# Moving the cross scores' maxima, two bfloat16 roundings and an output norm off ScalarE and VectorE

## The chip, the cores and the metric

The kernel runs on one core of a Trainium2 chip. Its five engines are TensorE (PE, whose weight loads are listed apart as PEld), VectorE (DVE), ScalarE (ACT), GpSimd (POOL) and SyncE (SP), which here only issues DMAs. The metric is device time in microseconds (us) of one launch; lower is better.

## The reference

One decoder layer with three sublayers, each followed by a residual and a layer norm, for 32 sequences ("batches") of 256 tokens by 256 features in float32:

```
x = layernorm(x + self_attention(x))         # 16 query heads of 64, 4 key/value heads, RoPE, ALiBi
x = layernorm(x + cross_attention(x, ctx))   # 16 heads of 16
x = layernorm(x + ffn(x))                    # bit-linear: weights in {-1, 0, 1}, activations rounded to 8 bits
```

Cross attention norms each of q, k, v and its own output before the projection (weight, bias), and lets each query see the keys of its own and the previous window of 64 that have the same cell id. Its heart, for one head:

```
p = where(mask, q @ k.T / sqrt(16), lowest)
a = exp(p - max(p)) / sum(exp(p - max(p)))
o = a @ v
y = (layernorm(o) * w + b) @ w_o.T + b_o
```

## The kernel before, in words

**Order of work.** Everything is unrolled in Python. Time is cut into slots of about 4 us, four to a group; a batch starts every 16 slots. In one group PE does two self-attention units of the current batch (scores L393, transposes L471, values L492) and one cross-attention unit of the batch before (scores L674, transposes L713, values L729, back-transposes L749). Generators (`self_inputs`, `self_output`, `cross_inputs`, `cross_output`, `feed_forward`) give the rest and yield until a later slot. For PE, DVE and ACT the program order is kept as written (`manual_schedule`); the order on POOL and on SP, which are not in that list, is made by the tile framework's scheduler when the program is built. Every engine works its own queue strictly in order.

**A cross unit.** Four heads lie in one 128x512 tile `xp`, and a unit has two such halves, with 128 queries and 128 keys for each head. DVE (L688) takes the scores from PSUM, adds the mask, negates, writes `xp` and gives each row's minimum to `xnm`, eight instructions to a unit. ACT (L704, `cross_exp`) then does one exponential for each head, with `xnm` as its bias operand and scale -1. PE transposes (L713), ACT copies (L715, `xpT`), PE multiplies with the values (L729); the value tiles have a column of ones, which gives the sum. There are four units to a batch.

**The queries of a cross unit** (`xqT`) come, for each half of the tokens, from `self_output`: PE `wo` (L513), DVE residual and statistics, POOL `rs_x` (L528 to L531), DVE `row` (L538), PE transposes (L204 `zqT`), projection (L550), ACT bias (L568 `qb`), an SP DMA that swaps neighbouring rows (L573), and POOL's rotation (L584, L585, L586). The keys `kTz` come by eight small SP DMAs (L658).

**Self attention's side jobs on DVE, POOL and SP.** The reciprocal sums are spread by a DVE copy `wide` (L443), a transposing SP DMA `planes` (L448) and a POOL copy `R` (L455). The rotary embedding needs four SP DMAs for each 128x512 tile (L312, `other<-psin`) and a POOL add (L354, `qT` or `kT`).

**Feed forward.** POOL scales and rounds (L803 `tr`, L852 `gu`), adding a large constant; DVE subtracts it again and writes bfloat16 (L805 `xib`, L855 `hib`); SP transposes by DMA (L809 `xiT`, L857 `hiT`); PE multiplies (L816, L863).

**Cross output.** DVE statistics of `on`, POOL `rstd_zo` (three small instructions, L184 to L186), ACT scales and shifts `on` (L198), PE transposes (L204 `zoT`) and multiplies with `xo_w` (L775), DVE adds the residual (L779).

Of the kernel before, what the change touches and what calls it, by code (L numbers as in the profile page):

```python
# [10 lines left out]
BF16 = mybir.dt.bfloat16  # L11
I32 = mybir.dt.int32
U16 = mybir.dt.uint16
AF = mybir.ActivationFunctionType
ALU = mybir.AluOpType
AX = mybir.AxisListType

P = 128
L = 256
NT = L // P  # L20
D = 256
NDC = D // P
EPS = 1e-5
# [7 lines left out]
XHH = 4  # L31
XE = XHD + 1
K_, V_, Q_, O_ = range(4)

INNER = 1024
# [3 lines left out]
MAGIC = 12582912.0  # L39
# [12 lines left out]
def kernel(  # L52
# [27 lines left out]
    nc = tc.nc  # L80
# [5 lines left out]
    def ctile(shape, dtype, name):  # L86
        return const.tile(shape, dtype, name=name, tag=name)
# [3 lines left out]
    def bank(name, shape=(P, 512), dtype=F32):  # L91
        return ps.tile(list(shape), dtype, tag="b", name=name)
# [4 lines left out]
    neg_half = ctile([P, 2], F32, "neg_half")  # L97
# [5 lines left out]
    def work(name, shape, bufs=2, dtype=F32):  # L103
        return sb.tile(list(shape), dtype, tag=name, name=name, bufs=bufs)

    def small(name, n):
        return sb.tile([P, 8], F32, tag="small", name=name, bufs=48)[:, 0:n]
# [36 lines left out]
    ones = ctile([P, P], F32, "ones")  # L144
# [10 lines left out]
    for i in range(2):  # L155


        t = ctile([P, (NT + 1) * XH * XE + 32 - XE], F32, f"xvaug{i}")
# [14 lines left out]
    def stats(src, name):  # L173

        st = small("st", 6)
        mv = small(f"mv_{name}", 2)
        nc.vector.bn_stats(st, src)
        nc.vector.bn_aggr(mv, st)
        return mv

    def rstd_of(mv, name):

        rb = small(f"rstd_{name}", 2)
        nc.gpsimd.tensor_scalar(rb[:, 0:1], mv[:, 1:2], EPS, None, ALU.add)  # L184
        nc.gpsimd.tensor_tensor(rb[:, 0:1], rb[:, 0:1], neg_half[:, 0:1], ALU.pow)
        nc.gpsimd.tensor_scalar(rb[:, 1:2], mv[:, 0:1], rb[:, 0:1], -1.0, ALU.mult, ALU.mult)  # L186
        return rb


    last = []  # L190
# [9 lines left out]
    def transposed(dst, src, name):  # L200

        pt = bank(name)
        for dc in range(NDC):
            nc.tensor.transpose(pt[:, dc * P : (dc + 1) * P], src[:, dc * P : (dc + 1) * P], ident)  # L204
        nc.scalar.copy(dst, pt[:, 0 : NDC * P].rearrange("p (c t) -> p c t", t=P))


    def prepare_cross():


        nc.sync.dma_start(vecs_sb, vecs)
        nc.sync.dma_start(cols_sb, cols)
        for j, (w, dst) in enumerate(
            (
                (wxk, xkv_w[:, :, 0:D]),
                (wxv, xkv_w[:, :, D : 2 * D]),
                (wxq, xq_w),
                (wxo, xo_w),
            )
        ):  # L220
            raw = work("tr", [P, NDC, D], 3)
            nc.sync.dma_start(raw, w.rearrange("(c p) n -> p c n", p=P))
            for dc in range(NDC):
                nc.gpsimd.tensor_scalar(
                    dst[:, dc, :], raw[:, dc, :], vecs_sb[:, j, 0, dc : dc + 1], None, ALU.mult
                )
            if j == 0:
                nc.sync.dma_start(wo_sb, Wo.rearrange("(c p) n -> p c n", p=P))
            if j in xbias:
                more = work("xp", [P, 512])  # L230
                row = more[:, 0:D]
                nc.sync.dma_start(row, rows[j].partition_broadcast(P))
                for dc in range(NDC):
                    nc.gpsimd.tensor_scalar(
                        more[:, D + dc * P : D + (dc + 1) * P],
                        ones,
                        vecs_sb[:, j, 1, dc : dc + 1],
                        None,
                        ALU.mult,
                    )  # L240
            yield 2
            pb = bank("mm")
            if j in xbias:
                for dc in range(NDC):
                    nc.tensor.matmul(
                        pb[:, 0:D],
                        more[:, D + dc * P : D + (dc + 1) * P],
                        raw[:, dc, :],
                        start=(dc == 0),
                        stop=(dc == NDC - 1),  # L250
                    )
                nc.vector.tensor_tensor(xbias[j], pb[:, 0:D], row, ALU.add)
            else:
                for ch in range(NDC):
                    for dc in range(NDC):
                        nc.tensor.matmul(
                            pb[:, ch : ch + 1],
                            raw[:, dc, ch * P : (ch + 1) * P],
                            vecs_sb[:, j, 1, dc : dc + 1],
                            start=(dc == 0),  # L260
                            stop=(dc == NDC - 1),
                        )
                nc.vector.tensor_tensor(xbcol[j], pb[:, 0:NDC], cols_sb[:, j, :], ALU.add)
            yield 2
# [401 lines left out]
    def cross_scores(b, i):  # L666
# [16 lines left out]
        for half in range(2):  # L683
            s["xp", i, half] = p = work("xp", [P, 512])
            for j in range(XHH):
# [10 lines left out]
                    s["xnm", i][half][:, j : j + 1],  # L696
                )

    def cross_exp(b, i, half):
        s = state[b]  # L700
        p = s["xp", i, half]
        for j in range(XHH):
            cols = slice(j * P, (j + 1) * P)
            nc.scalar.activation(  # L704
                p[:, cols], p[:, cols], AF.Exp, bias=s["xnm", i][half][:, j : j + 1], scale=-1.0
            )

    def cross_turn(b, i, half):
        s = state[b]
# [52 lines left out]
    def cross_output(b, t):  # L762
        s = state[b]
        on = s["on", t]
        mv = stats(on, "zo")
        rstd = rstd_of(mv, "zo")
        yield
        last.append(partial(scaled, on, on, rstd))
        yield 2
        zoT = work("zT", [P, NDC, P])  # L770
        transposed(zoT, on, "zoT")
        yield 2
        py = bank("xw")
        for dc in range(NDC):
            nc.tensor.matmul(py[:, 0:D], zoT[:, dc, :], xo_w[:, dc, :], start=(dc == 0), stop=(dc == NDC - 1))  # L775
        if t == 0:
            s["x2"] = work("x2", [P, NT, D])
        h = s["x2"][:, t, :]
        nc.vector.tensor_tensor(h, py[:, 0:D], s["x1", t], ALU.add)  # L779
        mv = stats(h, "x2")  # L780
        rstd = rstd_of(mv, "x2")
        yield
        last.append(partial(scaled, h, h, rstd))


    def feed_forward(b):
        x2 = state[b]["x2"]

        s = small("ffs", NT)
# [10 lines left out]
        xi = work("tr", [P, NT, D], 3)  # L800
        xib = work("xib", [P, NT, D], 1, BF16)
        for t in range(NT):
            nc.gpsimd.tensor_scalar(xi[:, t, :], x2[:, t, :], up[:, t : t + 1], MAGIC, ALU.mult, ALU.add)  # L803
        yield
        nc.vector.tensor_scalar(xib, xi, MAGIC, None, ALU.subtract)  # L805

        xiT = work("xiT", [P, NT, NDC, P], 1, BF16)
        for t in range(NT):
# [2 lines left out]
        gu = work("gu", [P, NT, INNER], 1)  # L811
# [14 lines left out]
        for t in range(NT):  # L826
            for half in range(2):
                pg = hidden("gate", t, half)
                cols = gu[:, t, half * 512 : (half + 1) * 512]
# [3 lines left out]
        for t in range(NT):  # L833
            for half in range(2):
                pg = hidden("up", t, half)
                cols = gu[:, t, half * 512 : (half + 1) * 512]
# [3 lines left out]
        for t in range(NT):  # L840

            m = small("ffm", 1)
            nc.vector.tensor_reduce(m, gu[:, t, :], AX.X, ALU.max, apply_absolute_value=True)
            sh = small("ffsh", 1)
            nc.vector.tensor_scalar(sh, m, u_of[:, t : t + 1], QUANT_MIN, ALU.mult, ALU.max)
            hup = small("ffhup", 1)
            nc.vector.reciprocal(hup, sh)
            nc.vector.tensor_scalar(hup, hup, u_of[:, t : t + 1], 127.0, ALU.mult, ALU.mult)
            d_of = small("ffd", 1)
            nc.vector.tensor_scalar(d_of, sh, ff_scale["down"], None, ALU.mult)  # L850
            d_ofs.append(d_of)
            nc.gpsimd.tensor_scalar(gu[:, t, :], gu[:, t, :], hup, MAGIC, ALU.mult, ALU.add)  # L852
            yield
            hib = work("hib", [P, INNER], 2, BF16)
            nc.vector.tensor_scalar(hib, gu[:, t, :], MAGIC, None, ALU.subtract)  # L855
            hiT = work("hiT", [P, NIC, P], 2, BF16)
            nc.sync.dma_start_transpose(hiT, hib)  # L857
            hiTs.append(hiT)
        yield 2
        for t in range(NT):  # L860
            py = bank("ffo")
# [6 lines left out]
            mv = stats(y, "y")  # L868
            rstd = rstd_of(mv, "y")
# [16 lines left out]
    at(-16, self_inputs(0))  # L886
    at(-16, prepare_buffers())
    at(-15, prepare_cross())
    at(2, prepare_ffn())
    for b in range(B):  # L890
        s0 = 16 * b
        if b:
            at(s0 - 15, self_inputs(b))
        at(s0 + 2, cross_inputs(b))
        for t in range(NT):
            at(s0 + 9 + 8 * t, self_output(b, t))
            at(s0 + 4 * CROSS + 11 + 8 * t, cross_output(b, t))
        at(s0 + 4 * CROSS + 26, feed_forward(b))

    with tc.manual_schedule(engines={mybir.EngineType.PE, mybir.EngineType.DVE, mybir.EngineType.Activation}):  # L900
        running = []
        slot = min(starts)
        while starts or running:
            m, part = divmod(slot, 4)
            k = m - CROSS
# [147 lines left out]
```

## Time and profile before

| what | value |
|---|---|
| median of 3 runs (lowest, highest) | 2186.22 us (2183.72, 2188.77) |
| span of the profiled execution, first to last instruction | 2184.1 us |
| busy: PE, DVE, ACT, POOL | 96%, 81%, 73%, 59% of the span |
| ACT: the cross exponentials L704 | 1024 of 416 ns, 331.8 us |
| DVE: `hib` L855 and `xib` L805 | 64 of 908 ns and 32 of 1384 ns |
| granted PE clock, mean | 0.983 |

The page gives no time of the profiled execution beside its span; the runs' median is 2.1 us above the span, and that is taken as what lies around it. Busy times are sums of instruction durations, so an instruction that waits for a port inside its duration counts as busy. In a timeline the columns are start, duration, engine, line, operation, output<-input with shapes, count, and in brackets the idle time before it with what ended that. Line numbers are those of the kernel before.

### The profile page before, as it was taken

How to read it: one execution, taken by the hardware profiler on the slowest of the kernel's cores; microseconds unless marked ns; L12 is line 12 of the kernel's file. 1: busy time of each engine (PE TensorE's matmuls, PEld its weight loads, DVE VectorE, ACT ScalarE, POOL GpSimd, SP SyncE). 2: the span in 40 equal slices, each digit the busy share in tenths (PEclk: the TensorE clock that was granted, in tenths of full speed). 3: DMA queues.
4: the chain of work that ended last, by engine and by line, in shares of the span. 5: the costliest groups of instructions: out<-in, count | busy, mean ns of one | idle time of the engine just before them, and what ended most of it. 6: DMA issues, size and time to landing. Idle time of an engine off the chain costs nothing.

```text
span 2184.1 us, 54367 instructions
## 1 busy us (share of the span) xinstructions
PE 2096.9 (96%) x17316; PEld 1606.7 (74%) x17316; DVE 1778.0 (81%) x6949; ACT 1600.0 (73%) x4833; POOL 1285.1 (59%) x1977
## 2 busy tenths in 40 slices
PE   7899999999999999999999999999999999999983
PEld 5677777777777777777777777777777777777751
DVE  4777888888888888888888888888888888888765
ACT  2478778777778877777877777877777877777862
POOL 4555665566655656655656655656666566666542
PEclk9899999999999999999999999999999999999986
DMA  7432333333333334334334333333343333333211
GB/s 219 111 75 72 82 75 83 77 79 86 89 72 78 83 71 91 86 71 86 76 76 89 82 77 79 78 81 83 86 82 76 81 82 74 90 81 69 53 42 32
DMA packets 326589, 177.57 MB, mean 81 GB/s; under 512 B 242976, under 2 KB 296096, under 8 KB 326304
## 3 DMA queue, kind: packets, MB, share of 16 engines
q1 hardware_dynamic: 324608, 170.52, 34.6%
q8 instruction: 139, 2.28, 0.5%
q10 hardware_dynamic: 1696, 3.57, 0.5%
q14 instruction: 146, 1.20, 0.2%
HBM read 39.50 MB, written 8.39 MB: 22 GB/s over the span
## 4 chain that ended last, share of the span: by engine, by line
PE 74%; DVE 11%; ACT 5%; POOL 4%; DMA 4%; issue 1%; SPq 0%; ACTq 0%; POOLq 0%; DVEq 0%
PE wo L513 10%; PE o L492 8%; PE proj L330 8%; PE t L471 8%; PE s L393 8%; PE ff L816 5%; PE xt L713 4%; PE xo L729 3%; PE xq L550 3%; PE xs L674 3%; PE ffo L863 3%; PE xk L622 3%; DVE p L409 2%; PE xw L775 2%; PE v L362 2%; DVE xib L805 2%
## 5 line engine op out<-in xcount | busy, mean ns | idle before, releaser
L427 ACT ACTIVATE p<-p,nm 128x256 f32<-128x256 f32 x1024 | 511.6, 512 | 197.7 <-DVE nm L409 197.7
L409 DVE CUSTOM_DVE_ANT_0 p<-s,alibi 128x256 f32<-128x256 f32 x1024 | 364.6, 416 | 6.3 <-PE s L393 6.3
L480 ACT COPY pT<-t 128x512 f32<-128x512 f32 x512 | 276.1, 601 | 89.6 <-PE t L471 89.3
L704 ACT ACTIVATE xp<-xp,xnm 128x128 f32<-128x128 f32 x1024 | 331.8, 416 | 0.0
L688 DVE CUSTOM_DVE_ANT_0 xp<-xs,mask 128x128 f32<-128x128 f32 x1024 | 225.9, 285 | 68.1 <-PE xs L674 68.1
L455 POOL COPY R<-planes 128x1024 uint16<-128x1024 uint16 x128 | 175.4, 1370 | 176.3 <-DMA planes<-wide 164.6
L471 PE MATMUL t<-ident,p 128*128 128x128 f32 x2048 | 266.4, 273 | 0.9 <-ACT p L427 0.9
L492 PE MATMUL o<-pT,v 128*64 128x256 f32 x2048 | 260.8, 386 | 1.3 <-ACT pT L480 1.1
L393 PE MATMUL s<-kT,qT 64*128 64x256 f32 x2048 | 255.7, 389 | 0.0
L513 PE MATMUL wo<-wo_sb,oT 128*128 128x256 f32 x1024 | 248.0, 386 | 0.4 <-ACT xpT L715 0.3
L354 POOL TENSOR_TENSOR qT<-qT,other 128x512 f32<-128x512 f32 x128 | 169.4, 1323 | 127.6 <-DMA other<-psin 66.4
L330 PE MATMUL proj<-xT,wq_sb 128*128 128x256 f32 x1024 | 243.1, 381 | 0.0
L471 PEld LDWEIGHTS t<-ident,p 128*128 128x128 f32 x2048 | 234.2, 141 | 9.4 <-ACT p L427 2.6
L393 PEld LDWEIGHTS s<-kT,qT 64*128 64x128 f32 x2048 | 187.3, 186 | 63.4 <-issue 14.3
L492 PEld LDWEIGHTS o<-pT,v 128*64 128x64 f32 x2048 | 143.9, 136 | 104.4 <-issue 21.2
L513 PEld LDWEIGHTS wo<-wo_sb,oT 128*128 128x128 f32 x1024 | 194.9, 193 | 30.9 <-ACT xpT L715 1.1
L427 ACT ACTIVATION_READ_ACCUMULATOR p<-p,nm 128x1 f32 x1024 | 208.0, 203 | 0.0
L330 PEld LDWEIGHTS proj<-xT,wq_sb 128*128 128x128 f32 x1024 | 185.8, 191 | 21.1 <-issue 0.4
L831 DVE SCALAR_TENSOR_TENSOR gu<-gu,ff 128x512 f32<-128x512 f32 x128 | 82.6, 684 | 84.5 <-ACT gu L830 84.3
L713 PEld LDWEIGHTS xt<-ident,xp 128*128 128x128 f32 x1024 | 110.6, 141 | 53.7 <-issue 38.5
L713 PE MATMUL xt<-ident,xp 128*128 128x128 f32 x1024 | 143.3, 281 | 2.1 <-ACT xp L704 2.0
L339 DVE TENSOR_TENSOR psin<-proj,rs_sb 128x512 f32<-128x512 f32 x160 | 109.8, 686 | 38.2 <-PE proj L330 34.6
(146 smaller groups left out, 4325.7 us busy)
## 6 DMA issues: line engine op xcount, KB each, us to landing
other<-psin SPq DMA_DIRECT2D x640, 64.0 KB, 2.0
xT<-in_xt_dram SPq DMA_DIRECT2D x32, 256.0 KB, 2.8
xs<-in_x_dram SPq DMA_DIRECT2D x32, 256.0 KB, 2.8
cs<-in_ctx_dram SPq DMA_DIRECT2D x32, 256.0 KB, 2.8
other<-qb SPq DMA_DIRECT2D x64, 128.0 KB, 2.1
kTz<-tr SPq DMA_DIRECT2D x256, 32.0 KB, 2.0
other<-qb SPq DMA_DIRECT2D x128, 64.0 KB, 2.0
out_dram<-x SPq DMA_DIRECT2D x32, 256.0 KB, 2.3
```

What stands on the lines that cost most here:

```text
L330: nc.tensor.matmul(pq[:, c * L : (c + 1) * L], w[:, dc, c * P : (c + 1) * P], xT[:, dc, :], start=(dc == 0), stop=(dc == NDC - 1),)
L393: nc.tensor.matmul(banks[half][:, rr * L : (rr + 1) * L], qT[rows_, rr, qc * P : (qc + 1) * P], kT[rows_, kc, :], start=(rr == 0), stop=(r ...
L409: nc.vector.tensor_tensor_reduce(p[:, cols], banks[half][:, cols], alibi[:, 2 * (4 * kc + 2 * rp + rr) + half, :], -0.125, 3.0e38, ALU.add ...
L427: nc.scalar.activation(p[:, cols], p[:, cols], AF.Exp, bias=nm[:, rr : rr + 1], scale=-1.0, accum_out=s["sums", i // 2][:, e : e + 1],)
L455: nc.gpsimd.tensor_copy(R.bitcast(U16).rearrange("p (n z) -> p z n", z=2), s.pop(("planes", m)).rearrange("p z r q -> p z (r q)"),)
L471: nc.tensor.transpose(pt[:, j * P : (j + 1) * P], p[half][:, rr * L + kk * P : rr * L + (kk + 1) * P], ident,)
L480: nc.scalar.copy(pT, pt)
L492: nc.tensor.matmul(po[half * HD : (half + 1) * HD, rp * L : (rp + 1) * L], s["v"][:, kk, (2 * kc + half) * HD : (2 * kc + half + 1) * HD], ...
L513: nc.tensor.matmul(py[:, 0:D], s["oT", qc, kc][:, r, :], wo_sb[:, 4 * kc + r, :], start=(kc == 0 and r == 0), stop=(kc == 1 and r == 3),)
L688: nc.vector.tensor_tensor_reduce(p[:, cols], banks[2 * half + j // 2][:, j % 2 * P : (j % 2 + 1) * P], s["mask"][:, qc, :], -1.0, 3.0e38, ...
L704: nc.scalar.activation(p[:, cols], p[:, cols], AF.Exp, bias=s["xnm", i][half][:, j : j + 1], scale=-1.0)
L713: nc.tensor.transpose(pt[:, j * P : (j + 1) * P], p[:, j * P : (j + 1) * P], ident)
```

## The change

Four things are changed. POOL subtracts the minima from `xp`, 128x512 in one instruction for each half, right behind DVE's scores, and ACT does one exponential of 128x512 with no bias in place of four of 128x128. POOL, and no longer DVE, subtracts the rounding constant and writes `xib` (two instructions of 128x256) and `hib` (one of 128x1024), `hib` one slot earlier in the program than before. The mean of cross output's norm is taken out of the weights: at the start, `xo_w` has its column means subtracted (two PE matmuls, two DVE instructions). Then `on` goes to PE unscaled, the ACT instruction that scaled it and the third POOL instruction of `rstd_zo` go, and DVE multiplies by `rstd_zo` in the residual add.

```diff
@@ prepare_cross
                 nc.vector.tensor_tensor(xbias[j], pb[:, 0:D], row, ALU.add)
+                if j == O_:
+                    for dc in range(NDC):
+                        nc.tensor.matmul(pb[:, D:], ones, dst[:, dc, :], start=(dc == 0), stop=(dc == NDC - 1))
+                    for dc in range(NDC):
+                        nc.vector.scalar_tensor_tensor(
+                            dst[:, dc, :], pb[:, D:], -1.0 / D, dst[:, dc, :], ALU.mult, ALU.add
+                        )
@@ cross_scores, cross_exp
+        for half in range(2):
+            p3 = s["xp", i, half].rearrange("p (h k) -> p h k", k=P)
+            nm = s["xnm", i][half].unsqueeze(2).to_broadcast([P, XHH, P])
+            nc.gpsimd.tensor_tensor(p3, p3, nm, ALU.subtract)
...
-        for j in range(XHH):
-            cols = slice(j * P, (j + 1) * P)
-            nc.scalar.activation(
-                p[:, cols], p[:, cols], AF.Exp, bias=s["xnm", i][half][:, j : j + 1], scale=-1.0
-            )
+        nc.scalar.activation(p, p, AF.Exp, scale=-1.0)
@@ cross_output
-        rstd = rstd_of(mv, "zo")
-        yield
-        last.append(partial(scaled, on, on, rstd))
-        yield 2
+        rstd = small("rstd_zo", 1)
+        nc.gpsimd.tensor_scalar(rstd, mv[:, 1:2], EPS, None, ALU.add)
+        nc.gpsimd.tensor_tensor(rstd, rstd, neg_half[:, 0:1], ALU.pow)
+        yield 3
...
-        nc.vector.tensor_tensor(h, py[:, 0:D], s["x1", t], ALU.add)
+        nc.vector.scalar_tensor_tensor(h, py[:, 0:D], rstd, s["x1", t], ALU.mult, ALU.add)
@@ feed_forward
+        for t in range(NT):
+            nc.gpsimd.tensor_scalar(xib[:, t, :], xi[:, t, :], MAGIC, None, ALU.subtract)
         yield
-        nc.vector.tensor_scalar(xib, xi, MAGIC, None, ALU.subtract)
...
             nc.gpsimd.tensor_scalar(gu[:, t, :], gu[:, t, :], hup, MAGIC, ALU.mult, ALU.add)
+            hib = work("hib", [P, INNER], 2, BF16)
+            nc.gpsimd.tensor_scalar(hib, gu[:, t, :], MAGIC, None, ALU.subtract)
             yield
-            hib = work("hib", [P, INNER], 2, BF16)
-            nc.vector.tensor_scalar(hib, gu[:, t, :], MAGIC, None, ALU.subtract)
```

In the program as built (its order of instructions on each engine, without times), PE, DVE and ACT keep their order apart from these edits. On POOL the two subtractions of a unit stand where the scheduler put them, once with a `qT` add between them. On SP the two `xiT` transposes stand ahead of the four `other<-psin` DMAs and the two `xvaug` copies that they followed before.

## The prediction

> **What bounds the kernel now.** I read the page first: its busy times, then its costliest groups, for who is full and what the touched instructions cost (share of the span; then busy us, mean ns, idle before).
>
> ```profile
> PE 2096.9 (96%) x17316; PEld 1606.7 (74%) x17316; DVE 1778.0 (81%) x6949; ACT 1600.0 (73%) x4833; POOL 1285.1 (59%) x1977
> ...
> L704 ACT ACTIVATE xp<-xp,xnm 128x128 f32<-128x128 f32 x1024 | 331.8, 416 | 0.0
> L354 POOL TENSOR_TENSOR qT<-qT,other 128x512 f32<-128x512 f32 x128 | 169.4, 1323 | 127.6 <-DMA other<-psin 66.4
> ```
>
> PE is all but full, so ACT and DVE time is worth only what PE waits for them. The PE timeline of one middle batch, 1031.8 to 1096.4 (first `xk` block to the next, 64.6 us), shows that wait.
>
> ```profile
> 1047.54 0.69 PE L674 MATMUL xs<-kTz,xqT 32*64 32x256 f32 x16
> 1048.62 0.91 PE L729 MATMUL xo<-xpT,xvaug 128*32 128x64 f32 x32 [0.39 <-ACT xpT L715]
> ...
> 1056.46 2.33 PE L492 MATMUL o<-pT,v 128*64 128x256 f32 x16
> ...
> 1062.33 0.71 PE L674 MATMUL xs<-kTz,xqT 32*128 32x256 f32 x8
> ```
>
> `xo` starts 0.39 late and takes 0.91 where the batch's other block of 32 takes 0.65 (1062.98); `o` takes 2.33 where its neighbours take 1.95 (1021.08, 1042.69). That is 0.39 + 0.26 + 0.38, about 1.05 us in a batch; waits of `zqT` for DVE `row` add some 0.2 in the mean. So the change can win at most about 1.2 us in each of 28 like batches, 34 us; the remaining waits lie at the start and the end.
>
> **What the change takes away.** Four exponentials of a half are issued 0.295 us apart (four end in 1.28 us, 1053.80). One of 128x512 without a bias lies between the 601 ns of the copy L480 and the 699 of the tanh L830, both 128x512; I take 0.65, so ACT wins some 0.6 us a half. The `on` scaling goes, 0.59 us twice a batch. DVE loses `xib` (1.48 at 1041.60) and two `hib` of 0.69 to 1.79. `xib` stands just ahead of the self scores whose exponentials hold `xpT` back, and the ACT relief comes just ahead of the `pT` copies that `o` waits for: all three PE waits above go. PE would then reach the 1062.33 block at about 1061.2.
>
> **What it adds on POOL.** Eight subtractions a batch at the 1.27 us of L354 (undelayed), two `hib` at the 1.12 of L852, two `xib` at the 0.47 of L803 (two end in 0.93, 1040.64), less 0.27 twice for `rstd_zo`: 10.2 + 2.2 + 0.9 - 0.5 = 12.8 us of POOL in 64.6, from 59% to some 79%. No sum says that this hurts; a chain does. It ends at `xqT`, for which the 1062.33 block waits. Here are POOL and then SP in that stretch before.
>
> ```profile
> 1045.50 1.27 POOL L354 TENSOR_TENSOR qT<-qT,other 128x512 f32<-128x512 f32 x1
> ...
> 1050.72 2.89 POOL L612 TENSOR_SCALAR mask<-ck_i,cq_sb 128x128 f32<-128x128 f32 x3 [2.80 <-DVE xnm L688]
> ...
> 1059.99 0.73 POOL L586 TENSOR_TENSOR xqT<-qb,other 128x256 f32<-128x256 f32 x1
> ```
>
> ```profile
> 1039.90 2.47 SPq L312 DMA_DIRECT2D other<-psin  x4
> ...
> 1043.74 2.49 SPq L809 DMA_TRANSPOSE xiT<-xib  x2
> ```
>
> I lay the changed order along these durations. The unit whose scores DVE starts at 1030.57 has its first half at 1031.5. Subtraction 1031.6 to 1032.9; `qT` held by DVE's `wide` (next part) to 1033.4, ends 1034.7; subtraction to 1036.05; three `rstd_y` to 1037.4; `R` 1.34 to 1038.8; four `rs_x` to 1040.5; L584 1.27 to 1041.75; `tr` to 1042.7; `xib` 0.1 + 0.94 to 1043.75. SP now issues `xiT` first, 1043.25 to 1045.75, and only then the four `psin` DMAs that before went out at 1039.90: to 1048.2, the last landing 2.0 after its issue, at about 1049.6. POOL, done with L585, L586 and `rstd_zo` at 1047.1, stands still until then. Then `qT` to 1051.0, the L540 add to 1051.7, two subtractions to 1054.3, mask and its add to 1058.0, `qT` to 1059.3, `R` to 1060.7, L584 to L586 with their gaps to 1063.0. Before, `xqT` was ready at 1060.72. PE gets it at 1063.1 instead of 1062.33: **0.75 us later a batch**, and the 1.1 won before has become part of a PE wait of 1.9 in one place. 28 batches give 21 us.
>
> Everything queued behind the subtractions on POOL shifts with them. The other `xqT` of the batch, ready at 1026.9 for 1029.71, comes some 1.2 later and still in time; `cs`, ready at 1026.3 for PE at 1027.36, comes about when it did, because DVE without `hib` reaches its scores earlier. ACT's first exponential there waits for the subtraction to 1053.0, before the 1053.80 of now, so that new wait on ACT costs nothing. `kTz` is a second chain: with `psin` moved, SP issues the last one at about the same 1060 as before, landing about 1062; it alone forbids PE much more than 0.3 us of gain there.
>
> **Ports.** DVE's `wide` follows the scores by 0.23 us, now while a subtraction runs. The combined timeline shows what that does.
>
> ```profile
> 1227.07 1.27 POOL L354 TENSOR_TENSOR qT<-qT,other 128x512 f32<-128x512 f32 x1 [1.66 <-DVE xnm L688]
> 1227.21 1.68 DVE L443 COPY wide<-rinv 128x1024 uint16<-128x1024 uint16 x1
> ```
>
> `wide` takes 0.69 alone and 1.68 here: it waits until POOL's add is nearly done. But beside the one-input mask (1050.72) a `wide` from 1050.77 takes 0.69. So I count 0.2 to 0.8 us for each `wide` behind a subtraction, hidden behind the `planes` DMA and a later slot except for the 0.5 above, and nothing for `hib` and `xib`. The Trainium skill's "Advanced Engine Details and Errata" (VectorE Performance Modes) says that GpSimd instructions and two-port Vector instructions block each other, without that distinction. By it `hib` would block as well, an estimate of 0.4 us more a batch, 11 us; the mask row speaks for my smaller count.
>
> **The clock.** The timeline near the end prices a long PE wait:
>
> ```profile
> 2060.94 0.93 PE L204 MATMUL zcT<-ident,cs 128*128 128x128 f32 x4 [2.15 <-ACT cs L198]
> 2061.71 3.48 PE L513 MATMUL wo<-wo_sb,oT 128*128 128x256 f32 x8
> ```
>
> After 2.15 us idle the granted clock (by windows) is 0.50 from 2061.85 to 2065.2, and `wo` takes nearly twice its 1.89 us (2068.96); after 1.04 idle (1241.35) it stays 1.00. My 1.9 lies nearer the upper row, but it is shorter, and before, small waits 14 us ahead are mixed in. I take one batch in five at half clock for 3.4 us, 1.7 us lost: 28 x 0.2 x 1.7 = 9.5 us; the ends are none and every batch (48 us). The Trainium skill's "TensorE: Matmul & The Clock Gate" (HAM oscillation) states its rule as no idle gaps above about 3.4 us; by it the 1.9 would cost nothing and the sum would be 9.5 less, but the 2.15 row contradicts it.
>
> **Start and end.** The start gets two PE matmuls (0.53 each, as L245) behind a DVE add, and two DVE instructions (0.48, as L867): 0 to 2 us, I take 1.5. At the end, `hib` is on the last chain twice, 1.12 for 0.70: +0.9; `xib` +0.1; the last exponentials about -0.8. The shorter `rstd_zo` is hidden behind feed forward. Together +2, between 0 and +5.
>
> **Sum.** 21 + 9.5 + 2 = 32.5 on the span of 2184.1, 2216.6; with the 2.1 around it, 2219.
>
> **Rivals.** *POOL keeps up, and it is faster.* If the chain to `xqT` is shorter by more than the 0.75 (the broadcast operand could be read faster than L354's; `psin` may land earlier than I lay it), PE is no later than now. The chain has 2.6 us of standing still in it, so it is not far off; `kTz` then limits it to about 0.3 to 0.5 a batch: 28 x 0.5 less, 2172. For it: POOL at 79% has room on average. Against: both queues come late at the same block. 16%. *The gain is just eaten* (`xqT` within 0.15 of now): 2186, 6%. *The clock falls in every batch*: the wait is 1.9, and the rows around 2.15 and 1.04 leave it open; 28 x (0.75 + 1.7) is 69, giving 2257. 25%. *My forecast*, POOL late and few clock falls, 53%. If the subtractions did not shorten ACT (one exponential of 128x512 as slow as four), the forecast would hold all the same, since ACT then isn't last.
>
> **Numbers.** A measurement of this kernel can tell about 0.2%, 4.4 us. Slower 0.78, same 0.06, faster 0.16. Range 2170 to 2275: below, the keeping-up case; above, the falling clock with 0.6 us more of chain.
>
> **What would show it.** Right: PE's L674 block, eight matmuls after the `o` block, idles 1.5 to 2.2 us a batch for `xqT`, POOL's `qT` waits over 2 us for `other<-psin` ahead of the second pair of subtractions, `xo` and `o` no longer wait, POOL is busy 77 to 80%, L704's successor takes 0.6 to 0.7. Wrong: a batch period under 64.6, `xqT` before PE asks, or subtractions far from 1.27.

## The result, and the profile after

The changed kernel takes 2289.07 us (median of 6 runs, 2282.76 to 2312.41) beside 2188.35 of the kernel before on the same chip (6 runs, 2183.72 to 2189.12). The ratio is 1.0485, with a 95% interval of 1.0451 to 1.0519: slower, some 101 us, three times what the prediction gave and above its range. The profiled execution has a span of 2291.1 us beside 2184.1, 107 more.

First the page of the changed kernel: its busy times, then the costliest groups with what the change touched, and `xib` from the list of groups by line (share of the span; busy us, mean ns, idle before). Line numbers from `prepare_cross` on are 7 to 9 higher than before.

```profile
PE 2128.8 (93%) x17258; PEld 1625.0 (71%) x17320; DVE 1758.8 (77%) x6855; ACT 1424.2 (62%) x4001; POOL 1761.1 (77%) x2297
...
L709 POOL TENSOR_TENSOR xp<-xp,xnm 128x512 f32<-128x512 f32 x256 | 286.2, 1133 | 43.8 <-DVE xnm L695 31.9
...
L863 POOL TENSOR_SCALAR hib<-gu 128x1024 bf16<-128x1024 f32 x64 | 178.2, 2784 | 5.2
L714 ACT ACTIVATE xp<-xp 128x512 f32<-128x512 f32 x256 | 169.6, 663 | 13.0 <-POOL xp L709 13.0
```

```profile
L813 POOL TENSOR_SCALAR xib<-tr 128x256 bf16<-128x256 f32 x64 | 54.5, 866 | 0.0
```

POOL at 77% and the exponential at 0.66 us are as forecast, the subtraction is a little cheaper (1.13 for 1.27). But `hib` takes 2.78 us where the sum had 1.12, and `xib` 0.87 where it had 0.47. The PE timeline of one batch shows two places of waiting.

```profile
1033.00 1.89 PE L520 MATMUL wo<-wo_sb,oT 128*128 128x256 f32 x8
1035.35 0.90 PE L681 MATMUL xs<-kTz,xqT 32*128 32x256 f32 x6 [0.47 <-POOL xqT L593]
1036.72 0.67 PE L681 MATMUL xs<-kTz,xqT 32*128 32x256 f32 x2 [0.47 <-DMA kTz<-tr]
...
1068.70 0.44 PE L204 MATMUL zcT<-ident,cs 128*128 128x128 f32 x2 [0.33 <-ACT cs L198]
1070.15 1.99 PE L520 MATMUL wo<-wo_sb,oT 128*128 128x256 f32 x8 [1.01 <-ACT xpT L723]
```

The **xs place** (1035.35) is the one that the prediction worked out. The **zcT place** (1068.70) is one that it had passed as free. From the trace, over 28 like batches, the times from the start of one PE block to the start of the next add up to 68.43 us a batch, 3.61 more than before:

| part of a batch | after less before, us |
|---|---|
| `wo` and `xs`, the xs place | +0.87 and +1.41 |
| the four `zcT` and the `wo` behind them | +1.70 and +0.08 |
| `xo`, `ff` and `wo` behind `xs`, at half clock in some batches | +0.87 |
| the old waits of `xo`, `o` and `zqT` | -1.30 |

The sums of the first two rows are 2.28 and 1.78. From the third batch's `xk` to the thirtieth's, 27 periods, the trace is 99 of the 107 us longer; the start, up to that third `xk`, differs by 0.4, and the end makes 9, of which 6.5 lie in the two periods up to the last `xk` and 2.2 behind it. What holds the zcT place is on POOL, and ACT shows who hands it on.

```profile
1059.79 1.12 POOL L861 TENSOR_SCALAR gu<-gu,ffhup 128x1024 f32<-128x1024 f32 x1
1060.99 0.22 POOL L184 TENSOR_SCALAR rstd_zc<-mv_zc 128x1 f32<-128x1 f32 x1
1061.29 2.79 POOL L863 TENSOR_SCALAR hib<-gu 128x1024 bf16<-128x1024 f32 x1
1064.04 0.57 POOL L185 TENSOR_TENSOR rstd_zc<-rstd_zc,neg_half 128x1 f32<-128x1 f32 x1
...
1067.74 0.27 POOL L186 TENSOR_SCALAR rstd_zc<-mv_zc,rstd_zc 128x1 f32<-128x1 f32 x1
```

```profile
1066.58 0.60 ACT L198 ACTIVATE cs<-cs,rstd_zc 128x256 f32<-128x256 f32 x1 [2.75 <-POOL rstd_zc L186]
1068.04 0.60 ACT L198 ACTIVATE cs<-cs,rstd_zc 128x256 f32<-128x256 f32 x1 [0.86 <-POOL rstd_zc L186]
...
1069.53 1.04 ACT L723 COPY xpT<-xt 128x512 f32<-128x512 f32 x2
```

The second `hib` stands between the first and the second instruction of `rstd_zc`. ACT waits 3.6 us in all for the two `rstd_zc`, and because it works in order, the copies of `xpT` queued behind `cs` are late too: that is PE's wait of 1.01 at `wo`. ACT's waits of this kind sum to 108.0 us, beside 10.4 before.

At the xs place the SP queue and the POOL queue show what the prediction had laid out: `xiT` ahead of `psin`, and POOL standing still for it. SP's waits for `xib` ahead of `xiT` sum to 226.8 us, in 31 times.

```profile
1085.08 2.46 SPq L818 DMA_TRANSPOSE xiT<-xib  x2
1087.63 2.47 SPq L319 DMA_DIRECT2D other<-psin  x4
```

```profile
1091.71 1.27 POOL L361 TENSOR_TENSOR qT<-qT,other 128x512 f32<-128x512 f32 x1 [2.26 <-DMA other<-psin]
```

After a wait at the xs place the clock falls in some batches. The timeline and the table by windows (PE, PEld, DVE, ACT and POOL busy, then the granted clock) of one of them:

```profile
1377.41 0.90 PE L681 MATMUL xs<-kTz,xqT 32*128 32x256 f32 x6 [0.97 <-POOL xqT L593]
...
1382.62 3.45 PE L520 MATMUL wo<-wo_sb,oT 128*128 128x256 f32 x8
```

```profile
1372.90:1378.90 6.00, 4.48 (x27) 3.45 (x26) 3.25 (x17) 3.70 (x14) 4.38 (x5) 1.00 0.20 41
1378.90:1385.70 6.80, 6.58 (x45) 4.43 (x47) 3.29 (x14) 0.97 (x2) 4.45 (x7) 0.50 0.29 56
```

`wo` takes 3.45 us for 1.89. Between 120 and 2040 us the trace has 14 stretches at clock 0.50, 54.6 us in all; the kernel before has none there. All 14 begin within 3 us behind a wait at the xs place, none behind the zcT place. They begin at whole multiples of 3.413 us from one another, to within 2 ns, and last 3.41 or 6.83 us; so how a wait lies to that grid may decide which batches are hit, which no run tested.

### The profile page after: what moved, and what is told of

Same layout as the page of the kernel before. It is cut to its first block, busy times and chain, and to the rows that moved or that the text cites. A ratio compares the mean times of both kernels' runs of the same rounds, so it can differ in the third digit from the quotient of the medians.

```text
span 2291.1 us, 54181 instructions
## 1 busy us (share of the span) xinstructions
PE 2128.8 (93%) x17258; PEld 1625.0 (71%) x17320; DVE 1758.8 (77%) x6855; ACT 1424.2 (62%) x4001; POOL 1761.1 (77%) x2297
## 3 DMA queue, kind: packets, MB, share of 16 engines
q8 instruction: 139, 2.28, 0.4%
## 4 chain that ended last, share of the span: by engine, by line
PE 76%; POOL 7%; DMA 5%; issue 3%; ACT 3%; DVE 3%; SPq 2%; ACTq 0%; another core or an unknown queue 0%; POOLq 0%; DVEq 0%
PE proj L337 10%; PE wo L520 9%; PE s L400 9%; PE o L499 9%; PE t L478 8%; PE xt L721 5%; PE ff L825 5%; PE xs L681 4%; PE xo L737 3%; PE xk L629 2%; PE xv L641 2%; PE xq L557 2%; DMA kTz<-tr 2%; PE ffo L872 2%; PE v L369 2%
## 5 line engine op out<-in xcount | busy, mean ns | idle before, releaser
L709 POOL TENSOR_TENSOR xp<-xp,xnm 128x512 f32<-128x512 f32 x256 | 286.2, 1133 | 43.8 <-DVE xnm L695 31.9
L520 PE MATMUL wo<-wo_sb,oT 128*128 128x256 f32 x1024 | 257.5, 396 | 28.4 <-ACT xpT L723 28.4
L499 PE MATMUL o<-pT,v 128*64 128x256 f32 x2048 | 253.0, 386 | 2.1 <-ACT pT L487 1.5
L520 PEld LDWEIGHTS wo<-wo_sb,oT 128*128 128x128 f32 x1024 | 202.2, 200 | 69.7 <-ACT xpT L723 35.0
L361 POOL TENSOR_TENSOR qT<-qT,other 128x512 f32<-128x512 f32 x128 | 175.5, 1371 | 92.0 <-DMA other<-psin 82.9
L499 PEld LDWEIGHTS o<-pT,v 128*64 128x64 f32 x2048 | 137.7, 137 | 102.3 <-issue 22.9
L863 POOL TENSOR_SCALAR hib<-gu 128x1024 bf16<-128x1024 f32 x64 | 178.2, 2784 | 5.2
L714 ACT ACTIVATE xp<-xp 128x512 f32<-128x512 f32 x256 | 169.6, 663 | 13.0 <-POOL xp L709 13.0
L746 ACT COPY xoT<-xo 128x256 f32<-128x256 f32 x128 | 47.6, 372 | 180.8 <-PE xo L737 179.9
L681 PE MATMUL xs<-kTz,xqT 32*64 32x256 f32 (+1 forms) x1536 | 118.2, 415 | 43.4 <-POOL xqT L593 29.3
```

The lines of the kernel that those rows point to most:

```text
L499: nc.tensor.matmul(po[half * HD : (half + 1) * HD, rp * L : (rp + 1) * L], s["v"][:, kk, (2 * kc + half) * HD : (2 * kc + half + 1) * HD], ...
L520: nc.tensor.matmul(py[:, 0:D], s["oT", qc, kc][:, r, :], wo_sb[:, 4 * kc + r, :], start=(kc == 0 and r == 0), stop=(kc == 1 and r == 3),)
L681: nc.tensor.matmul(banks[r][:, 0 : 2 * P].rearrange("p (h k) -> p h k", k=P)[q0:q1], s["xqT", qc][rows_, ch, q0:q1], kTz[rows_, ch, :, k0 ...
L709: nc.gpsimd.tensor_tensor(p3, p3, nm, ALU.subtract)
L863: nc.gpsimd.tensor_scalar(hib, gu[:, t, :], MAGIC, None, ALU.subtract)
```

## The experiments

Three accounts of the loss are put against each other. Theory "two places": the zcT place and the xs place are separate, each with a conversion next to it. Rival "POOL load": what counts is POOL's work in all. Rival "one place": only the zcT place counts, or its wait is given back at the next one. Times of a block below are means over 28 batches, from its start to the start of the next block, and "more than before" is against the kernel before. The kernel before is timed on the same chip in each set; it gave 2183.77, 2185.45 and 2185.97. A "changed kernel" below is the one of the diff, 2289.

### The output's type

```diff
-            hib = work("hib", [P, INNER], 2, BF16)
-            nc.gpsimd.tensor_scalar(hib, gu[:, t, :], MAGIC, None, ALU.subtract)
+            nc.gpsimd.tensor_scalar(gu[:, t, :], gu[:, t, :], MAGIC, None, ALU.subtract)
+            hib = gu[:, t, :].bitcast(BF16)[:, 0:INNER]
```

> The changed kernel with one thing altered: POOL's subtraction for hib writes float32 in place over gu, and the DMA transposes the first 2 KB of each row of that, so the feed forward multiplies other bits (its output is left wrong); every queue keeps its order. Theory 'two places': hib, 2784 ns on POOL instead of the 1120 of the prediction, stands in the middle of rstd_zc, on which ACT's cs scaling, the zcT block and wo wait (2.17 us instead of 0.44 for the four zcT matmuls, plus a later clock fall). Written as float32 it should take 1.1 us, the zcT block should fall to under 0.8 us and the time from 2289 to 2235 (2225 to 2250). Rival 'POOL load': what counts is POOL's work in all, 15.8 us a batch added for 104 us; 3.3 us less gives 2267. Rival 'one place': the wait ahead of zcT is given back at the next wait (xqT), no change, above 2280.

Measured 2286.86 us, ratio 1.0473 (1.0446 to 1.0500). The group of the altered line says why nothing moved:

```profile
L862 POOL TENSOR_SCALAR gu<-gu 128x1024 f32<-128x1024 f32 x64 | 178.4, 2787 | 5.2
```

It still takes 2.79 us, so the run decides nothing between the theories. It does strike out the explanation that I had taken for granted: writing bfloat16 is not what makes `hib` dear.

### hib back on DVE, xib back on DVE, no subtractions

Each is the changed kernel with one part of the diff undone.

> The changed kernel with hib back on DVE, where it stood before. 'Two places': the wait ahead of zcT and wo goes as with float32 hib, while DVE has 0.7 to 1.8 us twice a batch back: 2235 (2215 to 2250). 'POOL load': 5.6 of 15.8 us a batch less, 2252. 'One place': above 2275.

Measured 2251.34 us, ratio 1.0309 (1.0292 to 1.0326). The zcT block falls from 2.17 to 0.55 us, and the xs place stays (`wo` and `xs` 0.99 and 1.29 us more than before). The profiled execution has 68.3 us of half clock. By its number the run is nearest to "POOL load" (2252), just outside the range of "two places". But of the two places it is the zcT place that went, and only that. A batch is 0.90 us shorter than in the changed kernel and not the whole 1.62: `s` and `o` take 0.40 longer, and the blocks behind the xs place 0.30.

> The changed kernel with xib back on DVE; on SP the xiT transposes then stand behind the four psin DMAs again. 'Two places': the second place is xqT, 2.4 us of PE wait at the eight xs matmuls and the block ahead of them; POOL loses 1.73 us and the 2.3 us in which it stands still for psin, so xqT is in time, kTz leaves some 0.5 us, and the time is 2232 (2215 to 2250); the zcT wait stays. 'POOL load': 1.7 of 15.8 us less, 2278. 'One place' (only hib's counts, xqT's wait is hidden behind it): above 2280.

Measured 2245.01 us, ratio 1.0278 (1.0254 to 1.0303), near "two places" (2232) and far from "POOL load" (2278). The list of PE's waits (us in total, times, longest) has all but lost `xs` (6.9 us for 29.3), kept the zcT place (`wo` waits as long as in the changed kernel), and has the old wait of `xo` back:

```profile
PE wo L520 <- ACT xpT L723: 28.4, 28, 1.0
...
PE zcT L204 <- ACT cs L198: 17.4, 30, 2.5
PE xo L737 <- ACT xpT L723: 12.0, 30, 0.7
```

The last line is the prediction's reading that `xib` on DVE is what holds back `xpT`. Half clock is down to 13.7 us, four stretches, each right behind the zcT place.

> The changed kernel without the subtractions on POOL: four biased exponentials on ACT again; hib and xib stay on POOL. 'Two places': 2.5 us less of POOL ahead of each of the two places, both waits go or nearly, the old waits of xo and o (about 1.05 us a batch) come back: 2200 (2185 to 2220). 'POOL load': 9.0 of 15.8 us less, 2230. If hib alone were the cause, it would stay near 2270.

Measured 2261.18 us, ratio 1.0348 (1.0314 to 1.0382): neither theory. 9.0 of 15.8 us of POOL's added work are gone and only 26 us of time with them (against the 2286.86 of the same chip). The xs place keeps 0.50 and 1.56 us more than before, so 2.06 of 2.28. At the zcT place the four `zcT` take 1.14 us for 2.17: of 1.70 us, 1.03 went and 0.67 stays. So the subtractions, by far the largest addition to POOL, do little at the xs place and have a part in the zcT place, where a dear `hib` alone leaves 0.67. "POOL load" falls, since it had 2230; and "two places" had blamed the subtractions too much at the xs place.

### SP's order

```diff
-            nc.sync.dma_start_transpose(xiT[:, t, :, :], xib[:, t, :])
+            nc.scalar.dma_start_transpose(xiT[:, t, :, :], xib[:, t, :])
```

The yield ahead of it is 3 for 1 and the one behind it 1 for 3, so the slots of what follows are the same.

> The changed kernel with the two xiT transposes issued by ACT, two slots later, and no longer by SP ahead of psin; POOL's order and all else on SP unchanged. Theory 'SP order': at the second place xqT is late because SP stands before xiT, waiting for xib, with the four psin DMAs behind it. POOL's qT then waits no more (2.27 us before), xqT comes 2 us earlier, PE's wait at xs falls from 2.4 us to about 0.5, and the time from 2289 to 2240 (2225 to 2260), ACT paying some 2.4 us of issue a batch where it has room. Theory 'POOL time': xib's 1.73 us and the subtractions on POOL make it late, psin's place does not; no change, above 2280.

Measured 2225.82 us, ratio 1.0181 (1.0152 to 1.0209): 63 us back. The queues of SP and POOL at this place:

```profile
1052.45 2.46 SPq L319 DMA_DIRECT2D other<-psin  x4
1055.01 0.54 SPq L656 DMA_DIRECT2D xvaug<-xvaug  x1
```

```profile
1054.27 1.70 POOL L813 TENSOR_SCALAR xib<-tr 128x256 bf16<-128x256 f32 x2
...
1059.50 1.28 POOL L361 TENSOR_TENSOR qT<-qT,other 128x512 f32<-128x512 f32 x1
```

`psin` now goes out ahead of `xib`, 5.3 us earlier in the batch than in the changed kernel, `qT` waits for no `psin`, and of the xs place only 0.22 us at `xs` are left, though all of the change's work is still on POOL. SP's order made that place. Half clock is 13.7 us; three of its four stretches begin right behind the zcT place, which is still there.

### Both conversions on DVE, and the centred weights alone

> The changed kernel with hib and xib both back on DVE; subtractions, single exponential and centred weights stay. If the two places are independent, and each is caused by the conversion next to it, both waits go, 38 and 43 us: 2205, or less if the clock's falls go with them (2180 to 2210). If the subtractions alone are enough to make xqT or rstd_zc late, it stays above 2225.

Measured 2191.92 us, ratio 1.0036 (1.0024 to 1.0047). Both places are gone but for 0.19 us at `zcT`; the two single gains (36 and 42 us against 2286.86) would give 2209, and the clock's falls went with them (3.4 us left).

> The kernel before with the centred weights of cross output alone. ACT loses two instructions of 0.59 us a batch and POOL two of 0.27, DVE's residual add becomes 0.48 instead of 0.42. The waits of xo (0.7 with its tail) and o (0.37) for ACT could go in part: 2175 (2165 to 2187). If ACT's time there is not what those waits hang on: 2184 to 2187, plus up to 2 at the start.

Measured 2178.70 us, ratio 0.9969 (0.9958 to 0.9980). A small gain. The difference of these two kernels is the subtractions with the single exponential: here they cost 13 us. They do take away the wait of `o` (its block takes 2.19 us without them, 1.88 with them), but the block ahead of `zqT` takes 1.63 us with them and 0.98 without: `zqT` comes late for it.

### What the slow instruction is

> The kernel before, with twenty instructions of the disputed kinds appended behind its end, twice each, most on POOL and 128x1024. hib took 2787 ns also with float32 output, so the type of the output is out. Theory 'subtract': the subtraction from a constant is the slow one; every tensor_scalar with subtract takes 2.8 us, those with add or multiply 1.1. Theory 'one operation': instructions with one operation take 2.8 us whatever it is, those with two take 1.1. Theory 'constant': those whose first scalar is a constant and not a column take 2.8. The form multiply by a column of ones, then add or subtract the constant, into bfloat16, tells whether hib can be had for 1.1 us. The 128x512 subtraction of two tiles: 1.03 as L709 undelayed, the add of the same form 1.27 as L361.

The instructions stand behind the kernel's end and were profiled in one execution. Rows by line, POOL, mean ns: multiply by a column and add the constant into float32 (L976), subtract, add and multiply alone (L977 to L979), multiply and add constants (L980), multiply and subtract constants (L981), then into bfloat16 subtract alone (L984), multiply by a column and add (L986), plain copy (L988).

```profile
L976 POOL TENSOR_SCALAR gu<-gu,pc 128x1024 f32<-128x1024 f32 x2 | 2.2, 1120 | 0.1
L977 POOL TENSOR_SCALAR gu<-gu 128x1024 f32<-128x1024 f32 x2 | 5.6, 2782 | 0.0
L978 POOL TENSOR_SCALAR gu<-gu 128x1024 f32<-128x1024 f32 x2 | 5.6, 2784 | 0.1
L979 POOL TENSOR_SCALAR gu<-gu 128x1024 f32<-128x1024 f32 x2 | 5.5, 2774 | 0.1
L980 POOL TENSOR_SCALAR gu<-gu 128x1024 f32<-128x1024 f32 x2 | 2.1, 1047 | 0.1
L981 POOL TENSOR_SCALAR gu<-gu 128x1024 f32<-128x1024 f32 x2 | 7.3, 3630 | 0.1
...
L984 POOL TENSOR_SCALAR hib<-gu 128x1024 bf16<-128x1024 f32 x2 | 5.6, 2779 | 0.1
L986 POOL TENSOR_SCALAR hib<-gu,pc 128x1024 bf16<-128x1024 f32 x2 | 2.2, 1120 | 0.0
L988 POOL CAST hib<-gu 128x1024 bf16<-128x1024 f32 x2 | 2.1, 1035 | 0.0
```

None of the three theories of that run is right as it stood. The only quick `tensor_scalar` forms tried are multiply, then add, with a column or a constant, into either type: 1.05 to 1.12. One operation alone costs 2.77 to 2.85, whichever it is; multiply, then subtract costs 3.63 to 3.72. So `hib` can be had for 1.05 us as multiply by 1.0, then add minus the constant. The 128x512 subtraction of two full tiles took 1.26, like the add; with the second input a broadcast column, as in the change, 1.04.

### The change at the assumed prices

```diff
-            nc.gpsimd.tensor_scalar(hib, gu[:, t, :], MAGIC, None, ALU.subtract)
+            nc.gpsimd.tensor_scalar(hib, gu[:, t, :], 1.0, -MAGIC, ALU.mult, ALU.add)
```

> The changed kernel with hib on POOL as multiply by 1.0, then add minus the constant (1.12 us or less in the probe) in place of the subtraction (2.78); every queue keeps its order. Theory 'price': hib's place on POOL does no harm at 1.12, the zcT block falls from 2.17 us to under 0.7 and the time as far as with hib on DVE, to 2250 (2240 to 2260); the wait for xqT stays. Rival 'place': the new instruction between the three of rstd_zc makes them late whatever it costs; 2275 or more.

Measured 2220.86 us, ratio 1.0160 (1.0133 to 1.0188), with every queue in the order of the changed kernel. The row of `hib`, and PE's wait for `cs` in the changed kernel and in this one:

```profile
L863 POOL TENSOR_SCALAR hib<-gu 128x1024 bf16<-128x1024 f32 x64 | 66.8, 1044 | 5.2
```

```profile
PE zcT L204 <- ACT cs L198: 14.9, 31, 2.5
```

```profile
PE zcT L204 <- ACT cs L198: 1.8, 2, 1.0
```

One instruction's price, 2.78 against 1.04, is worth 68 us, more than expected. The zcT wait is gone, and with it PE's wait at the `wo` behind it, with the place of `hib` on POOL kept; so "price" stands and "place" falls. It beats `hib` on DVE by 30 us: there DVE spent 1.44 us on each.

> The changed kernel with hib and xib both as multiply and add on POOL, all queues in the same order: the change at the prices that the prediction assumed. If its sum failed by the two prices alone, this gives the 2219 of the sum (2205 to 2235): the zcT wait gone, xib 0.8 us less ahead of xqT, but SP still standing for xib ahead of psin, so 1 to 1.5 us of PE wait at xs stays. If the sum was wrong elsewhere too, it lands outside; above 2240 if the wait at xs and the clock's falls do not shrink.

The second edit is the same for `xib`, now 0.41 us. Measured 2208.58 us, ratio 1.0102 (1.0085 to 1.0119): the change as the prediction had priced it, and within its range. The xs place keeps 0.82 and 1.18 us more than before. The profiled execution is the slowest of the four, 2216.25 us; the others took 2207.46 to 2208.64.

> The changed kernel with both repairs: multiply and add for hib and xib, and the xiT transposes issued by ACT. The run with ACT's xiT alone had left 1.72 and 0.24 us a batch at zcT and the wo behind it, 55 us in all, and 13.7 us of half clock: 2168 (2158 to 2180), below the kernel before. If POOL's load is still too much for its order, 2190 or more.

Measured 2143.60 us, ratio 0.9806 (0.9791 to 0.9820): faster than the kernel before, and by more than was expected. The PE timeline at the xs place, and the page:

```profile
1042.78 0.38 PE L520 MATMUL wo<-wo_sb,oT 128*128 128x256 f32 x1
1043.09 0.71 PE L681 MATMUL xs<-kTz,xqT 32*128 32x256 f32 x8
```

```profile
PE 2067.8 (97%) x17320; PEld 1596.7 (75%) x17320; DVE 1708.8 (80%) x6855; ACT 1423.6 (67%) x4001; POOL 1627.5 (76%) x2297
```

POOL is as busy (76%) as in the kernel that lost 101 us (77%). There is no half clock between 120 and 2040 us, and a batch takes 63.70 us. In the mean over the batches `xs` still takes 0.30 us more than before.

> The same without the subtractions: four biased exponentials again. If the subtractions bring something (xo and o no longer wait for ACT), 8 to 15 us slower than with them: about 2180. If they cost what the comparison of the kernel with both conversions on DVE and the kernel with centred weights alone says (13 us), it is the faster one: about 2157.

Measured 2151.75 us, ratio 0.9844 (0.9830 to 0.9859). Here the subtractions with the single exponential win 8 us, where they cost 13 with the conversions on DVE: without them the wait of `o` is back (0.32 us a batch, less 0.21 that `xs` gains), and some 6 us more lie at the end. What that part is worth depends on the rest of the change: how POOL's queue makes the difference was not followed further.

## Why the prediction was wrong

**The step that failed** is the price of `hib` and `xib`: "two `hib` at the 1.12 of L852, two `xib` at the 0.47 of L803". Those rows have the shapes but not the operation: both are multiply, then add, and the moved instruction is a lone subtraction. It measured 2.78 and 0.87. The trace before had rows of a lone operation, at the start of the kernel, which the prediction did not use: two lone multiplications (L224, L234) beside L803.

```profile
L224 POOL TENSOR_SCALAR xo_w<-tr,vecs_sb 128x256 f32<-128x256 f32 x2 | 1.8, 922 | 0.0
L234 POOL TENSOR_SCALAR xp<-ones,vecs_sb 128x128 f32<-128x128 f32 x4 | 2.4, 604 | 0.0
...
L803 POOL TENSOR_SCALAR tr<-x,ffup 128x256 f32<-128x256 f32 x64 | 29.9, 480 | 0.0
```

L224 takes 0.92 us on the shape for which L803 takes 0.48, and so near what `xib` took. From L234 to L224 a further 128 columns cost 0.32; carried on to 1024 columns that gives 2.8 us, an estimate, and near what `hib` took. At the assumed prices the change takes 2208.6, 10 below the forecast of 2219; the two prices together cost 80 us, 68 of them `hib`'s. The prediction set no upper bound for either.

**What followed from it**: "`cs` ... comes about when it did". With `hib` at 2.78 the zcT place cost 1.78 us a batch; at 1.05 it costs nothing. The subtractions have a part in it: without them some 0.7 is left. The prediction had looked at DVE there, and not at how long POOL's queue is ahead of the last instructions of `rstd_zc`.

**The chain to `xqT`** was right. The run at the assumed prices has 2.00 us more than before at the xs place (forecast 1.9) and 1.24 less at the old waits (forecast 1.1), so 0.76 net for 0.75. `xiT` ahead of `psin`, and POOL idle for it (2.26 us for 2.6), was the cause there, as the run with `xiT` on ACT shows; the subtractions in that chain mattered less than they looked (2.06 of 2.28 us stay without them). `xo` and `o` no longer wait, from the causes named: `xib` off DVE for `xo`, the single exponential for `o`. So nearly all that the prediction had named as a sign of being right was seen, with the time 70 us off: none of its signs looked at `hib` or at the zcT place.

**The clock** was undersized for the change: 0.34 us a batch forecast, 0.87 measured. At the assumed prices it is 0.68 (44.4 us at half clock) in the profiled execution. But that one had a mean granted clock of 0.975, the other three 0.979 to 0.981; if start and end are alike in them, an estimate by these figures is 0.3 to 0.4 there, near the forecast. By the runs most falls go with the xs place: 44 to 68 us of half clock in the runs that have it, 13.7 or less in those that do not. The zcT place can make the clock fall too: with the xs wait gone, all four stretches with `xib` on DVE and three of four with `xiT` on ACT begin right behind it. The wait at the xs place is some 2 us, which the row of 2.15 had shown to be enough. The Trainium skill's "TensorE: Matmul & The Clock Gate" (HAM oscillation) would have allowed it, with its rule of no gaps above about 3.4 us; the windows above contradict that for this kernel.

**Start and end** were forecast at 2 us more. In the change the start is 0.4 us shorter and what follows the last `xk` 2.2 longer, so that was about right; the other 6.5 of the 8 us outside the 27 periods are the two periods behind them. At the assumed prices the profiled execution is 8 us shorter than before outside the 27 periods, nearly all of it behind the last `xk` (108.1 us for 116.9). In the median run there, 10 us below the forecast, this is then the term that misses; what made the end shorter stays open.

**Ports.** "Nothing for `hib` and `xib`" was wrong for `hib`. The combined timeline:

```profile
1053.35 2.79 POOL L863 TENSOR_SCALAR hib<-gu 128x1024 bf16<-128x1024 f32 x1
...
1055.19 1.49 DVE L450 COPY wide<-rinv 128x1024 uint16<-128x1024 uint16 x1
```

`wide` beside `hib` took 1.48 to 1.50 us in 28 of 29 cases, 0.55 past the end of `hib`. The mask row, by which the prediction took it that an instruction with one input does not block, was read from `wide` alone. Here are the masks of 128x128 before, where `wide` runs beside 30 of the 32, and after, where it runs beside none:

```profile
L612 POOL TENSOR_SCALAR mask<-ck_i,cq_sb 128x128 f32<-128x128 f32 x32 | 39.6, 1239 | 84.4 <-DVE xnm L688 84.2
```

```profile
L619 POOL TENSOR_SCALAR mask<-ck_i,cq_sb 128x128 f32<-128x128 f32 x32 | 23.6, 738 | 3.2
```

The 30 took some 1.27 us, the two without `wide` 0.72 and 0.74. So there it is POOL's instruction that takes longer, and the two do hinder each other. The Trainium skill's "Advanced Engine Details and Errata" (VectorE Performance Modes), which makes no distinction, fits both rows. What the longer `wide` cost by itself was not tried.

**The rivals.** Of the forecast's cases the falling clock (2257) came nearest in number and was not the cause. The time of "POOL keeps up" (2172) was reached, and passed, only by another kernel, the one with both repairs (2143.6).

## What to carry to other kernels

Price a moved instruction by a row with the same operation, not only the same shape; look for one in the whole trace, the start of the kernel too, and where there is none, keep the range open upward, or measure the instruction by itself. Before an engine takes on work in a strict queue, look for what stands behind the new instruction: here a norm's tiny instructions, with ACT's queue behind them. The new instruction's place there was harmless at 1.04 us and cost 1.78 us a batch at 2.78. An in-order DMA queue that waits for a late producer holds back everything behind it, and issuing that one DMA elsewhere brought back 63 us with no less work on the busy engine.

## What the hardware showed that was not expected

POOL's `tensor_scalar` on 128x1024 takes 1.05 to 1.12 us as multiply, then add, but 2.77 to 2.85 with one operation and 3.63 to 3.72 as multiply, then subtract, to float32 or bfloat16 alike. DVE did the same lone subtraction into bfloat16 in 0.85 us in the same run, behind the kernel's end. The Trainium skill's "GPSIMD Engine Reference" (Engine selection) calls one-input instructions roughly line-rate on GpSimd; the copy (1.04) and multiply, then add fit that beside DVE's 0.85, the lone operations do not.
